# A gated delta-rule layer on one core: the last head pair's output projection, its loads and its buffers

## The chip, the cores and the metric

The kernel runs on 1 core of one Trainium2 chip. The time is the device time of one execution in microseconds (us). All data is float32.

## The reference

The layer normalizes `x` (2 sequences of 2048 tokens, 512 features) and adds three things: `x` itself, an attention part and a mixture of experts on the first 512 tokens. The change is in the attention part, which is a gated delta rule with 16 heads of 128 features:

```
q, k, v = silu(conv4(xn @ Wq)), silu(conv4(xn @ Wk)), silu(conv4(xn @ Wv))
alpha, beta = sigmoid(xn @ Wa + ba), sigmoid(xn @ Wb + bb)
for t:                                       # for every sequence and head
    err = S @ k[t] - v[t]
    S = alpha[t] * S - beta[t] * outer(err, k[t])
    o[t] = S @ q[t]
o = layernorm(o) * ln_w + ln_b
o = o * sigmoid(xn @ Wg)
out = x + o.reshape(T, 16 * 128) @ Wo + experts
```

## The kernel before

**Tiling.** A sequence is cut into 16 chunks of 128 tokens, four chunks make a block of 512. The heads are taken in pairs, eight pairs for each of the two sequences. The recurrence of a pair runs over the 16 chunks in order; within a chunk it is matrix products (a triangular inverse, products with the state S).

**Steps.** `recurrence(b, first)` runs over all chunks of all pairs of sequence `b`, and two steps more at the end to drain what is begun. In each step it weaves generators together by hand, `step(g)` advancing one of them: `before` (chunk m: scores, inverse; L614 loads, L625 scores), `after` (chunk m-1: L687 state times keys, L698, L707, state L714, outputs L721 and L724), `output` (chunk m-2: layer norm, transposition L753, gate, L759, and at L761 the store of the pair's outputs to `oT_d[b][ci]`), and the projections q, v and g of the next block (`item`, matmuls L155, convolution L141). In all but the last two pairs of the second sequence it also prepares the keys of the pair after next (`key_item`). In the last pair there are no keys, and in its last block no projections either.

**Order.** In the recurrence TensorE, VectorE, ScalarE and GpSimd keep the order that is written. The DMAs, issued by SyncE's queue (SP), are ordered by a scheduler by when they are expected to be ready; SP issues them one after another and stands still where one has to wait. The product `qg` on GpSimd (L388) reads `gin`, loaded at L380 into one buffer.

**Output projection.** All heads of a chunk, stored by the eight pairs in `oT_d[b][ci]` (128 x 16 x 128, 1 MB), are multiplied by Wo: 16 matmuls of 128x512 that add up in one PSUM bank, in four groups of four heads (each matmul is two instructions in the profile, so a group is x8). VectorE adds `x` (the tile `xf`), and the sum is stored in `out`. For the first sequence this runs behind its recurrence, for the second within the last pair's steps: at step ci of the last pair, from ci = 4 on, `out_chunk(b, ci - 4, ...)` issues the loads of `oTf` (L880) and `xf` (L882) and gives the four groups (L892) to the step, the first of them near its start. The tile `oTf` is a buffer of the ring that held the transposed input, `xT`, four buffers; one becomes free for it at ci = 4, one more at 8 and at 12:

```
if c == 0:
    slots.append(big())
...
last = out_chunk(b, ci - 4, wos, slots[ci % len(slots)])
```

Chunks 12 to 15 come behind the last step. The weights Wo take other buffers that are free by then (`load_wo`): two of the three of the ring `xA`, one of `xT`, and those of keys and inverses.

## Time and profile before

| what | us |
|---|---|
| median of 3 runs | 3907.49 |
| lowest, highest | 3904.68, 3910.8 |
| the profiled execution | 3906.37 |
| its span, first to last instruction | 3904.3 |
| last pair's step 4 (the first with outputs) begins | 3547.6 |
| last L687 (state times keys) | 3838.59 |
| last sum (L895) | 3900.56 |

The profile is of one execution. Engines are PE (TensorE's matmuls; PEld its weight loads), DVE (VectorE), ACT (ScalarE), POOL (GpSimd) and SP. A line of the timeline has the start and the duration in us, the engine, the line of the program, the operation, what it writes and reads, how many instructions are merged, and in brackets how long the engine was idle before and what ended that. PEclk is the TensorE clock that was granted, as a share of full speed. A line of the windows has the stretch, its length, and each engine's busy time with the number of its instructions.

### The profile page before, as it was taken

Reading aid. Unit: us, or ns where it says so; the run is one execution under the profiler, and the core shown is the slowest. Engines: PE = TensorE matmul, PEld = TensorE weight load, DVE = VectorE, ACT = ScalarE, POOL = GpSimd, SP = SyncE. Lnnn points to the kernel's source line nnn. Section 1 sums busy time; section 2 is a strip of 40 time slices with the busy share of each in tenths; the row PEclk is TensorE's granted clock in tenths of the full one; section 3 lists DMA queues with packets and bytes.
Section 4 is the critical chain, followed back from the end, with each engine's and each line's share of the span. In section 5 each row is a group of like instructions: output and inputs, shape, how many; then the busy total and the mean of one; then the engine's idle time right before and its main releaser. Section 6 shows DMA issues by size and latency. Waiting matters only on the chain.

```text
span 3904.3 us, 59006 instructions
## 1 busy us (share of the span) xinstructions
PE 3770.2 (97%) x18046; PEld 2461.4 (63%) x18046; DVE 2343.6 (60%) x6132; ACT 1701.5 (44%) x4027; POOL 1682.4 (43%) x3046
## 2 busy tenths in 40 slices
PE   7769999999999999999999999999999999998899
PEld 6437767677677766666654466666666666664454
DVE  5536656666666667777750177777777777763231
ACT  3424444444444445555520055555555555542110
POOL 1236546465564636363630053636363545541010
PEclk7789999999999999999999999999999999999999
DMA  4634665655666553545573435353435444342322
GB/s 133 209 98 143 185 169 154 195 158 175 168 176 172 159 178 107 143 132 169 147 240 117 120 103 137 107 139 109 132 111 139 119 127 126 103 111 72 100 75 89
DMA packets 579705, 541.36 MB, mean 139 GB/s; under 512 B 354688, under 2 KB 421760, under 8 KB 574272
## 3 DMA queue, kind: packets, MB, share of 16 engines
q1 hardware_dynamic: 557280, 456.18, 40.6%
q0 software_dynamic: 22112, 81.41, 7.1%
q8 instruction: 147, 2.41, 0.3%
q14 instruction: 166, 1.36, 0.1%
HBM read 363.69 MB, written 173.67 MB: 138 GB/s over the span
## 4 chain that ended last, share of the span: by engine, by line
PE 85%; DVE 6%; DMA 4%; issue 2%; POOL 2%; SPq 1%; ACT 1%; POOLq 0%; DVEq 0%; ACTq 0%
PE p L155 39%; PE p L892 11%; PE p L1044 4%; DVE cv L141 3%; PE o L721 3%; PE l L625 3%; PE p L205 3%; PE o L724 3%; PE c L698 3%; PE c L707 3%; PE c L687 2%; PE p L1059 2%; PE l L640 1%; PE l L658 1%; PE l L667 1%
## 5 line engine op out<-in xcount | busy, mean ns | idle before, releaser
L141 DVE SCALAR_TENSOR_TENSOR cv<-raw,prm,cv 128x512 f32<-128x512 f32 x1152 | 909.5, 790 | 106.2 <-ACT cv L136 44.1
L892 PE MATMUL p<-wo,oTf 128*128 128x512 f32 x1024 | 459.7, 604 | 26.3 <-DMA oTf<-oT_d 25.1
L155 PE MATMUL p<-xT,wq 128*128 128x512 f32 x1024 | 484.6, 596 | 0.0
L653 POOL COPY inv<-iT 32x32 f32<-32x32 f32 x512 | 103.1, 201 | 884.4 <-DVE iT L645 685.1
L155 PE MATMUL p<-xT,wg 128*128 128x512 f32 x1024 | 482.0, 594 | 0.0
L155 PE MATMUL p<-xT,wv 128*128 128x512 f32 x1024 | 481.0, 593 | 0.0
L735 POOL TENSOR_TENSOR rs<-rs,mhalf 128x2 f32<-128x2 f32 x256 | 270.2, 1055 | 485.4 <-DVE rs L734 481.1
L132 ACT COPY raw<-p 128x512 f32<-128x512 f32 x384 | 223.4, 582 | 533.2 <-PE p L155 515.0
L155 PE MATMUL p<-xT,wk 128*128 128x512 f32 x896 | 433.5, 610 | 0.0
L702 ACT COPY w<-c 128x256 f32<-128x256 f32 x256 | 95.3, 372 | 635.0 <-PE c L698 635.0
L714 DVE SCALAR_TENSOR_TENSOR S<-S,gtot,c 128x128 f32<-128x128 f32 x480 | 145.2, 344 | 356.6 <-PE c L707 342.5
L892 PEld LDWEIGHTS p<-wo,oTf 128*128 128x128 f32 x1024 | 193.9, 194 | 252.2 <-issue 223.8
L267 POOL TENSOR_TENSOR Y<-Y,t 128x30 f32<-128x30 f32 (+14 forms) x480 | 308.4, 643 | 37.2
L136 ACT ACTIVATE cv<-p,prm 128x512 f32<-128x512 f32 x384 | 300.4, 782 | 1.7
L264 POOL TENSOR_TENSOR t<-Y 128x30 f32<-128x30 f32 (+14 forms) x480 | 286.2, 596 | 8.8 <-DMA Y<-aT_d 2.3
L155 PEld LDWEIGHTS p<-xT,wq 128*128 128x128 f32 x1024 | 178.0, 192 | 135.8 <-issue 135.8
L155 PEld LDWEIGHTS p<-xT,wg 128*128 128x128 f32 x1024 | 176.8, 191 | 132.3 <-issue 132.1
L155 PEld LDWEIGHTS p<-xT,wv 128*128 128x128 f32 x1024 | 176.3, 191 | 132.0 <-issue 132.0
L691 DVE SCALAR_TENSOR_TENSOR r<-c,gd,kv 128x128 f32<-128x128 f32 x480 | 145.3, 344 | 166.2 <-PE c L687 165.1
L155 PEld LDWEIGHTS p<-xT,wk 128*128 128x128 f32 x896 | 160.6, 198 | 126.3 <-issue 126.3
L388 POOL TENSOR_TENSOR qg<-q,gin 128x512 f32<-128x512 f32 x128 | 194.1, 1516 | 98.6 <-ACT q L386 98.6
L707 PEld LDWEIGHTS c<-w,kg 128*128 128x128 f32 x1024 | 154.1, 191 | 121.4 <-issue 102.1
(172 smaller groups left out, 7145.8 us busy)
## 6 DMA issues: line engine op xcount, KB each, us to landing
row<-a_d SPq DMA_DIRECT2D x128, 258.0 KB
dec_d<-decA SPq DMA_DIRECT2D x128, 258.0 KB
decB<-dec_d SPq DMA_DIRECT2D x64, 516.0 KB
k_d<-kf SPq DMA_DIRECT2D x128, 256.0 KB
k<-k_d SPq DMA_DIRECT2D x64, 512.0 KB
gin<-gin_d SPq DMA_DIRECT2D x128, 256.0 KB
aT_d<-aTf SPq DMA_DIRECT2D x128, 256.0 KB
oT_d<-oT SPq DMA_DIRECT2D x256, 128.0 KB
```

Of the source, the lines that this page charges most:

```text
L132: nc.scalar.copy(raw[:, KS - 1:], ps)
L136: nc.scalar.activation(cv, ps, AF.Identity, bias=cbias(p, h0 + h), scale=tap(p, h0 + h, KS - 1))
L141: nc.vector.scalar_tensor_tensor(cv, raw[:, j:j + BLK], tap(p, h, j), cv, ALU.mult, ALU.add)
L155: nc.tensor.matmul(ps, lhsT=w[:, k, h * D:(h + 1) * D], rhs=xt[k], start=(k == 0), stop=(k == NKT - 1))
L264: nc.gpsimd.tensor_tensor(t, bass.AP(col.tensor, col.offset, [col.ap[0], (Q, j), (0, n)]), bass.AP(row.tensor, row.offset, [row.ap[0], (0, ...
L267: nc.gpsimd.tensor_tensor(Y[:, 0:j, j + 1:], Y[:, 0:j, j + 1:], t, ALU.add)
L388: nc.gpsimd.tensor_tensor(qg[:, h, :], qt[:, h, :], gin, ALU.mult)
L691: nc.vector.scalar_tensor_tensor(r[:, h, :], pq[:, h * D:(h + 1) * D], gd0[b][:, ci, h0 + h:h0 + h + 1], kv[:, 1, h, :], ALU.mult, ALU.add)
L707: nc.tensor.matmul(pss[:, h * D:(h + 1) * D], lhsT=kg[:, h, :], rhs=w[:, h, :], start=True, stop=True)
L735: nc.gpsimd.tensor_tensor(rs, rs, mhalf[:, 0:HG], ALU.pow)
L892: nc.tensor.matmul(py, lhsT=oT[:, h, :], rhs=wos[h], start=(h == 0), stop=(h == H - 1))
L1044: nc.tensor.matmul(ps[:fn, s, :], lhsT=w[f][:, s, k, :], rhs=xt[:, k, :], start=(k == 0), stop=(k == NKT - 1))
```

## The change

Three things are changed. First, the loads of a chunk's outputs and of its `x` are taken out of `out_chunk` into a function `get_out`, which is called one step earlier: at step ci, from ci = 3 on, it asks for chunk ci - 3, and the matmuls of chunk ci - 4 are given to the step. Second, there are two buffers in turn from the start: for even chunks three pieces (`pieces`: 8 heads in the third buffer of `xA`, and twice 4 heads in the two buffers of `decA`, which held the decay matrices of keys), each loaded by its own DMA; for odd chunks the tile `big` as before. Third, the two draining steps take chunks 12 and 13, and only chunks 14 and 15 come behind the last step. The first sequence's outputs use the same functions with one whole tile, in the order of before.

```diff
-                    if u == NB * NP - 1:
-
-                        if ci == 1:
-                            wos = load_wo(b)
-                        if ci >= 4:
-                            if c == 0:
-                                slots.append(big())
-                            for _ in last:
-                                pass
-                            last = out_chunk(b, ci - 4, wos, slots[ci % len(slots)])
-                            step(last)
                 A, B = pair
                 ps = None
+                if m >= len(steps) - NC and b == NB - 1:
+
+                    ci = m - len(steps) + NC
+                    if ci == 1:
+                        wos = load_wo(b)
+                    if ci == 3:
+                        slots.append(pieces())
+                    if ci == 4:
+                        slots.append([(big(), H)])
+                    for _ in last:
+                        pass
+                    last = none
+                    if ci > 3:
+                        last = out_chunk(b, ci - 4, wos, *got)
+                    if ci >= 3:
+                        got = get_out(b, ci - 3, slots[(ci - 3) % 2])
...
         if slots:
-            for ci in range(NC - 4, NC):
-                for _ in out_chunk(b, ci, wos, slots[ci % len(slots)]):
-                    pass
+            for c in range(NC - 2, NC):
+                if c > NC - 2:
+                    got = get_out(b, c, slots[c % 2])
+                drain(out_chunk(b, c, wos, *got))
...
-    def out_chunk(b, c, wos, oT):
-
-        nc.sync.dma_start(out=oT, in_=oT_d[b][c])
+    def pieces():
+
+        return [(half("oTa", [P, 8, C]), 8),
+                *((ap.tile([P, 4, C], F32, tag="decA", name="oTa", bufs=2), 4) for _ in range(2))]
+
+    def get_out(b, c, parts):
+
+        heads = []
+        for t, n in parts:
+            o = len(heads)
+            nc.sync.dma_start(out=t, in_=oT_d[b][c][:, o:o + n, :])
+            heads += [t[:, h, :] for h in range(n)]
         xin = ap.tile([P, HID], F32, tag="aTf", name="xf", bufs=2)
         nc.sync.dma_start(out=xin, in_=x[b, c * C:(c + 1) * C, :])
+        return heads, xin
+
+    def out_chunk(b, c, wos, heads, xin):
+
...
-        yield
         py = bank(ps_p, "p")
         for h in range(H):
-            nc.tensor.matmul(py, lhsT=oT[:, h, :], rhs=wos[h], start=(h == 0), stop=(h == H - 1))
+            nc.tensor.matmul(py, lhsT=heads[h], rhs=wos[h], start=(h == 0), stop=(h == H - 1))
```

More of the change, by code (lines that the diff above doesn't have):

```diff
@@ L899, in block_kernel @@
     recurrence(0, p0)
-    slots = [big() for _ in range(NBK - 1)]
+    slots = [[(big(), H)] for _ in range(NBK - 1)]
     wos, first = load_wo(0), projection(NP * NBK)
     for c in range(NC):
-        for _ in out_chunk(0, c, wos, slots[c % 3 if c < 12 else 1 + c % 2]):
-            pass
+        drain(out_chunk(0, c, wos, *get_out(0, c, slots[c % 3 if c < 12 else 1 + c % 2])))
         if c > 12:
```

## The prediction

> **What bounds the kernel now.** I read the page's busy shares and chain first, then TensorE's waits in the last 400 us, then that stretch cut at the chunks of the last pair, then TensorE's and SP's timelines there. The page:

> ```profile
> PE 3770.2 (97%) x18046; PEld 2461.4 (63%) x18046; DVE 2343.6 (60%) x6132; ACT 1701.5 (44%) x4027; POOL 1682.4 (43%) x3046
> PE 85%; DVE 6%; DMA 4%; issue 2%; POOL 2%; SPq 1%; ACT 1%; POOLq 0%; DVEq 0%; ACTq 0%
> L892 PE MATMUL p<-wo,oTf 128*128 128x512 f32 x1024 | 459.7, 604 | 26.3 <-DMA oTf<-oT_d 25.1
> ```

> TensorE is 97% busy and 85% of the chain that ended last, so time comes out only by removing TensorE work or its gaps. The output projection (L892) has idle time of its own: 26.3 us, 25.1 of it for the load of oTf. The waits of TensorE from 3540 us on say how many gaps these are:

> ```profile
> PE p L892 <- DMA oTf<-oT_d: 25.1, 6, 9.0
> ```

> Six gaps. To find what one costs with all that follows from it, I cut the last pair from the score product (first L625) of one chunk to that of the next:

> ```profile
> core 0: us, PE busy (x) PEld busy (x) DVE busy (x) ACT busy (x) POOL busy (x), PEclk, DMA share, GB/s
> 3547.60:3580.83 33.23, 24.23 (x81) 12.81 (x80) 6.45 (x20) 4.91 (x12) 3.73 (x7) 0.85 0.19 60
> 3580.83:3612.62 31.79, 26.64 (x90) 14.02 (x88) 7.59 (x23) 4.81 (x12) 3.86 (x8) 0.95 0.24 72
> 3612.62:3639.15 26.53, 23.31 (x81) 12.44 (x80) 6.45 (x20) 4.74 (x12) 1.90 (x5) 0.94 0.16 60
> 3639.15:3670.56 31.41, 26.73 (x90) 14.03 (x88) 7.58 (x23) 4.86 (x12) 2.46 (x6) 0.95 0.32 91
> 3670.56:3696.62 26.06, 23.31 (x82) 12.45 (x80) 6.46 (x20) 4.69 (x12) 3.54 (x6) 0.93 0.35 126
> 3696.62:3721.40 24.78, 24.78 (x90) 13.30 (x88) 7.58 (x23) 4.81 (x12) 3.67 (x7) 1.00 0.24 84
> 3721.40:3742.76 21.36, 21.36 (x82) 11.79 (x80) 6.47 (x20) 4.74 (x12) 1.71 (x4) 1.00 0.21 71
> ```

> The rows are chunks 4 to 10. Chunks 9 and 10 are solid: length equals TensorE's busy time, granted clock 1.00. They are the measure of a step without a gap: 24.78 us with two projection items (odd chunks), 21.36 with one (even). Chunks 4 to 8 do the same work in 26 to 33 us, at clocks of 0.85 to 0.95. No other engine is near full (DVE 7.6 of 25). Inside chunk 5, and in chunk 9 without the wait:

> ```profile
> 3580.83 0.69 PE L625 MATMUL l<-q,k 128*128 128x128 f32 x4
> 3586.67 5.29 PE L892 MATMUL p<-wo,oTf 128*128 128x512 f32 x8 [5.15 <-DMA oTf<-oT_d]
> 3591.80 1.88 PE L155 MATMUL p<-xT,wq 128*128 128x512 f32 x4
> ...
> 3696.62 0.69 PE L625 MATMUL l<-q,k 128*128 128x128 f32 x4
> 3697.15 3.60 PE L892 MATMUL p<-wo,oTf 128*128 128x512 f32 x8
> 3700.58 1.88 PE L155 MATMUL p<-xT,wq 128*128 128x512 f32 x4
> ```

> The wait is 5.15 us, and the eight matmuls behind it take 5.29 instead of 3.60. L625 to L155 takes 10.97 us against 3.96: 7.01 lost, two thirds of it idle and the rest slow clock. SP shows why some chunks wait and others don't:

> ```profile
> 3580.44 0.34 SPq L880 DMA_DIRECT2D oTf<-oT_d  x1
> 3699.05 0.33 SPq L882 DMA_DIRECT2D xf<-in_x  x1
> 3699.67 0.32 SPq L880 DMA_DIRECT2D oTf<-oT_d  x1
> ```

> Chunk 5's load leaves SP at 3580.44, when its one buffer has just come free, and TensorE wants it at 3581.5; 1 MB needs until 3586.7. From chunk 8 on there are more buffers: the load issued at 3699.67 is for chunk 10, whose outputs begin at 3721.9, 22 us later.

> **The change, part by part.**

> *Five gaps.* The load for the outputs of chunk ci-4 is now asked at step ci-1, into the other of two buffers. The first buffer is an 8-head piece (the third xA buffer) and two 4-head pieces (decA, which keys no longer use); the second is the tile that was the only one at steps 4 to 7. What goes is what each step has above the solid ones: 33.23 - 21.36 = 11.87; 31.79 - 24.78 = 7.01; 26.53 - 21.36 = 5.17; 31.41 - 24.78 = 6.63; 26.06 - 21.36 = 4.70. Sum 35.4 us: 24.8 of idle (9.00 + 5.15 + 3.22 + 4.68 + 2.75) and 10.6 of slow clock.

> *Clock, row and rule.* The rows have the slow clock behind all five gaps, also those of 3.22 and 2.75 us. [...] These very matmuls are in the trace, so I take the row.

> *Are the new loads in time?* Even chunks: heads 0 to 7 and 8 to 11 wait only for TensorE to be done with the same piece two chunks earlier (mid-step), heads 12 to 15 for the last pair's store of that chunk, issued at the step's end. Odd chunks: 1 MB, asked just behind that store. All are wanted one step later, 17.9 us at the least (the steps without projections, L625 at 3767.53 and 3785.44). The longest comparable load is the one of 7.2 us (issue 3550.08, matmul 3557.28). Cost taken: nothing, under a cover of over 10 us.

> *A new wait on SP.* Before, the load at step ci read a chunk stored a full step earlier; now it reads one stored just before. [...] The trace has this wait at the end:

> ```profile
> 3856.97 0.32 SPq L761 DMA_DIRECT2D oT_d<-oT  x1
> 3859.35 0.32 SPq L880 DMA_DIRECT2D oTf<-oT_d  x1
> ```

> 2.4 us, with SP stopped in it. Were it on the path in each of 13 chunks, it would take 31 us and leave 9 of the gain. But SP stops there already: xf waits 2.0 us for the store of out (3697.0 to 3699.05) in the same place, so the two overlap. Queued behind are inv for a chunk three steps on, gin and, twice, a block's operands. gin issued at 3579.17 feeds the POOL product at 3607.95, 29 us later. Cost taken: 0; bounds 0 and 31.

> *SP's extra issues.* Eight even chunks are three DMAs instead of one: 16 issues of 0.33 us, 5.3 us of SP in 300. Two of chunk 0's pieces move some pairs ahead, since those heads are stored then; each may hold SP for up to 2.4 us among key and operand loads, in stretches where TensorE has no wait. Cost 0; bounds 0 and 10. The bytes are the same. TensorE's order of instructions is unchanged up to the last chunk, and so is POOL's to the end.

> *The end.* Before, chunks 12 to 15 came behind the recurrence, and the two draining steps ran bare:

> ```profile
> 3840.34 0.68 PE L698 MATMUL c<-r,inv 128*128 128x128 f32 x4 [1.14 <-DVE r L691]
> ```

> From L687 at 3838.59 to the last matmul's end at 3900.5 is 61.9 us. The work in it, at the full clock's pace: 128 matmuls x 0.43 = 55.0; L687, L698 and L707 0.44 each; L721/L724 0.89; two L753 0.44. Sum 57.7. The change puts chunk 12's and 13's matmuls between the links of these chains, as the solid steps have them, so I take the difference, 4.2 us. What is late next there is chunk 15's load: its outputs are stored behind chunk 13's sum, 34.1 us after that L687 (chunks 12 and 13 27.5, three heads of chunk 14 that stand ahead 2.6, the links 2.7, the sum on DVE 0.7, the outputs' own last product 0.4, SP 0.2); the store ends at 36.6, the load lands 5.5 to 6.5 later at 42.1 to 43.1, and TensorE wants it at 43.9. In time by about 1 us; cost 0, bounds 0 and 4 (a gap with its slow clock).

> *Sum.* 35.4 + 4.2 = 39.6 us off a span of 3904.3: 3864.7. The profiled execution took 3906.37, 2.1 above its span: 3866.8. The median 3907.49 is 1.1 above that execution: 3867.9 us, 1.0% less than before.

> **The rivals.**

> *The loads come late in part.* SP takes its instructions in order, and the pieces wait for TensorE in mid-step. If half the gaps survive at 3 us with the slow clock behind (6 x 2.5 = 15 us), or chunk 15 is late and SP's holds show, the gain is 20 to 28 us: 3880 to 3888. For it: the 1 us margin at the end. Against: covers of over 10 us everywhere else. 12%.

> *It doesn't do what it says.* If each load were held until its step begins, only the 4.2 us at the end remain: 3903, no change. Against: the buffer asked for has been free since the step before, and the store that it waits for comes a whole step ahead of the use. 3%.

> *Slower, by POOL.* gin stands behind the pieces on SP. If it lands after POOL has reached the product qg, POOL stands still with the copies into inv and kg behind it, and L698 and L707 wait for those. A late gin can cost a step, up to 25 us, and three of them lie in this stretch: 75 - 40 = 35 us slower, 3943. It decides once gin is later than its use, that is, over 26 us later than now; the pieces hold SP for 14 at most, to the third group of outputs. 5%.

> **How the numbers follow.** The forecast has 80%, the rivals 12, 3 and 5. About 0.2% (7.8 us) is what a measurement of this kernel can tell from no change. Faster: 80 + 12 = 92%; same 3%; slower 5%. The low end is the forecast less the scatter of the runs shown, twice its 3 us above and below their median, and less 2 for gaps sized too small: 3860. The high end takes in the end's 4 us, SP's 10 and the near part of the first rival: 3884.

> **What would show it.** The chunks 4 to 8 of the last pair at 21.4 and 24.8 us in turn, clock 1.00; no TensorE wait on oTf or the pieces; loads issued a step ahead, about 2.7 us after each step's store of out; from the last chunk's L687 to the end of the matmuls some 58 us. Wrong would be: waits of L698 or L707 on POOL, a piece's load as TensorE's releaser, a gap before chunk 15, or a stretch ahead of 3540 us that changed its length.

## The result and the profile after

The changed kernel takes 3866.95 us (median of 4 runs, 3865.86 to 3868.41) against 3907.44 us before (4 runs, 3904.68 to 3910.8): a ratio of 0.9898, with a 95% interval of 0.9882 to 0.9914. The forecast was 3867.9. The span of the profiled execution went from 3904.3 to 3864.4 us. From the page after, its busy shares, its chain by engine and the output projection (now L910):

```profile
PE 3759.2 (97%) x18046; PEld 2457.7 (64%) x18046; DVE 2343.3 (61%) x6132; ACT 1701.4 (44%) x4027; POOL 1681.2 (44%) x3046
PE 85%; DVE 5%; issue 2%; DMA 1%; ACT 1%; POOL 0%; SPq 0%; POOLq 0%; ACTq 0%; DVEq 0%
L910 PE MATMUL p<-wo,oTf 128*128 128x512 f32 x768 | 335.1, 592 | 0.0
```

The number of matmuls is the same and TensorE is busy for 11.0 us less: the same instructions ran faster. The group's idle time of 26.3 us is 0.0, and DMA went from 4% of the chain to 1%. (The other 256 instructions read the pieces, `oTa`, and are a group of their own.) The steps 4 to 8 of the last pair (the prediction's "chunks 4 to 8"; the outputs made in them are those of chunks 0 to 4), cut at the score products as before; the first columns are the stretch, its length and TensorE's busy time, and PEclk is the granted clock:

```profile
core 0: us, PE busy (x) PEld busy (x) DVE busy (x) ACT busy (x) POOL busy (x), PEclk, DMA share, GB/s
3547.29:3568.64 21.35, 21.35 (x82) 11.78 (x80) 6.45 (x20) 4.92 (x12) 3.73 (x7) 1.00 0.42 132
3568.64:3593.42 24.78, 24.78 (x90) 13.30 (x88) 7.58 (x23) 4.81 (x12) 3.86 (x8) 1.00 0.19 63
3593.42:3614.76 21.34, 21.34 (x81) 11.77 (x80) 6.45 (x20) 4.74 (x12) 1.90 (x5) 1.00 0.32 109
3614.76:3639.54 24.78, 24.78 (x89) 13.30 (x88) 7.59 (x23) 4.86 (x12) 2.46 (x6) 1.00 0.32 86
3639.54:3660.89 21.35, 21.35 (x81) 11.78 (x80) 6.45 (x20) 4.69 (x12) 3.54 (x6) 1.00 0.39 139
```

In all five TensorE has no gap: length equals busy time, clock 1.00. They take 113.60 us against 149.02 before, 35.42 less. The whole difference of the spans can be laid out so. Ahead of step 4, 3547.60 became 3547.29, 0.3 less. Steps 4 to 8 give 35.4. From step 9 to the last L687 it is 141.97 us in both, no difference. From that L687 to the end of the span, 65.7 became 61.5, 4.2 less. Sum 39.9.

At the end, chunk 12's groups stand between the links of the last chain (L698, L707), which had waited for DVE and ACT before, and the chunks follow with no wait:

```profile
3802.86 0.61 PE L687 MATMUL c<-S,k 128*128 128x128 f32 x4
3803.31 3.60 PE L910 MATMUL p<-wo,oTa 128*128 128x512 f32 x8
3806.74 0.61 PE L698 MATMUL c<-r,inv 128*128 128x128 f32 x4
3807.19 3.60 PE L910 MATMUL p<-wo,oTa 128*128 128x512 f32 x8
3810.62 0.61 PE L707 MATMUL c<-w,kg 128*128 128x128 f32 x4
...
3835.58 11.32 PE L910 MATMUL p<-wo,oTa 128*128 128x512 f32 x26
3846.74 13.90 PE L910 MATMUL p<-wo,oTf 128*128 128x512 f32 x32
```

On SP the new waits are there, and no TensorE wait follows from them: from 3540 us to the end the profile shows no wait of TensorE. SP's own waits in the last pair from 3540 us on, for the loads of outputs (L894) and of `x` (L897):

```profile
SPq L894 <- PE l L667: 37.1, 6, 6.8
SPq L894 <- PE p L910: 29.9, 8, 5.3
SPq L897 <- DMA out<-xf: 16.6, 14, 2.4
SPq L894 <- DMA oT_d<-oT: 1.8, 8, 0.4
```

The columns are the total, the number of times and the longest. SP stands still for 67 us until TensorE has moved on (31.9 us in before, for L880). By the program a piece can be loaded only when TensorE has read the one before it in the same buffer. The profile names an output product (L910) for 29.9 us of this; for 37.1 us it names L667, a product that stands next to an output group. The wait that the forecast had bounded at 31 us, for the store of the outputs just made, is 1.8 us in all: SP has already stood for the store of `out` in the row above it.

### The profile page after: what moved, and what is told of

It reads as the page before. It is cut to its first block, busy times and chain, and to the rows that moved or that the text cites. A ratio compares the mean times of both kernels' runs of the same rounds, so it can differ in the third digit from the quotient of the medians.

```text
span 3864.4 us, 59038 instructions
## 1 busy us (share of the span) xinstructions
PE 3759.2 (97%) x18046; PEld 2457.7 (64%) x18046; DVE 2343.3 (61%) x6132; ACT 1701.4 (44%) x4027; POOL 1681.2 (44%) x3046
## 4 chain that ended last, share of the span: by engine, by line
PE 85%; DVE 5%; issue 2%; DMA 1%; ACT 1%; POOL 0%; SPq 0%; POOLq 0%; ACTq 0%; DVEq 0%
PE p L155 40%; PE p L910 11%; PE p L1061 4%; DVE cv L141 3%; PE o L721 3%; PE l L625 3%; PE p L205 3%; PE o L724 3%; PE c L698 3%; PE c L707 3%; PE c L687 3%; PE p L1076 2%; PE l L658 1%; PE l L640 1%; PE l L667 1%
## 5 line engine op out<-in xcount | busy, mean ns | idle before, releaser
L155 PE MATMUL p<-xT,wq 128*128 128x512 f32 x1024 | 482.7, 594 | 0.0
L155 PE MATMUL p<-xT,wg 128*128 128x512 f32 x1024 | 482.0, 594 | 0.0
L155 PE MATMUL p<-xT,wv 128*128 128x512 f32 x1024 | 481.0, 593 | 0.0
L155 PE MATMUL p<-xT,wk 128*128 128x512 f32 x896 | 436.4, 613 | 0.0
L910 PE MATMUL p<-wo,oTf 128*128 128x512 f32 x768 | 335.1, 592 | 0.0
L155 PEld LDWEIGHTS p<-xT,wq 128*128 128x128 f32 x1024 | 177.4, 191 | 134.4 <-issue 134.4
L155 PEld LDWEIGHTS p<-xT,wg 128*128 128x128 f32 x1024 | 176.8, 191 | 132.3 <-issue 131.9
L155 PEld LDWEIGHTS p<-xT,wv 128*128 128x128 f32 x1024 | 176.3, 191 | 132.0 <-issue 132.0
L910 PEld LDWEIGHTS p<-wo,oTf 128*128 128x128 f32 x768 | 143.5, 190 | 168.8 <-issue 168.6
L691 DVE SCALAR_TENSOR_TENSOR r<-c,gd,kv 128x128 f32<-128x128 f32 x480 | 145.2, 344 | 168.7 <-PE c L687 167.4
L155 PEld LDWEIGHTS p<-xT,wk 128*128 128x128 f32 x896 | 162.2, 199 | 128.6 <-issue 128.6
L707 PEld LDWEIGHTS c<-w,kg 128*128 128x128 f32 x1024 | 154.3, 191 | 121.2 <-issue 101.4
```

The costliest lines, as they stand in the source:

```text
L155: nc.tensor.matmul(ps, lhsT=w[:, k, h * D:(h + 1) * D], rhs=xt[k], start=(k == 0), stop=(k == NKT - 1))
L691: nc.vector.scalar_tensor_tensor(r[:, h, :], pq[:, h * D:(h + 1) * D], gd0[b][:, ci, h0 + h:h0 + h + 1], kv[:, 1, h, :], ALU.mult, ALU.add)
L707: nc.tensor.matmul(pss[:, h * D:(h + 1) * D], lhsT=kg[:, h, :], rhs=w[:, h, :], start=True, stop=True)
L910: nc.tensor.matmul(py, lhsT=heads[h], rhs=wos[h], start=(h == 0), stop=(h == H - 1))
```

## The experiments

They ran in three rounds, each on a chip of its own, and each with the kernel before beside it. Its medians are 3903.38 us (round 1: the late call, the two ends, the filled waits), 3904.06 us (round 2: one buffer, the waits filled in part, each load twice) and 3905.66 us (round 3: the changed kernel). Differences are taken to the kernel before of the same round. The changed kernel takes 40.4 us less than before in its round; where a kernel of another round is set against it, the 2 us between the chips are in the comparison.

**The changed kernel once more, and the loads called for in the step of use.** The first is unchanged; the second has this edit (and its like behind the loop):

```diff
                     if ci > 3:
+                        got = get_out(b, ci - 4, slots[ci % 2])
                         last = out_chunk(b, ci - 4, wos, *got)
-                    if ci >= 3:
-                        got = get_out(b, ci - 3, slots[(ci - 3) % 2])
```

> The changed kernel itself once more, on the chip of the experiments, as their measure. Theory A (the calling place of the loads is worth nothing, the difference between the two chips is the same for both kernels): as the kernel with the loads called for in the step that uses them, 3864 us within 2, and 39 to 40 less than before on the same chip. Rival (asking ahead in the program is worth a few microseconds beyond the second buffer): 3861 or less.

> The changed kernel, with the loads called for in the step that uses them, as before; the two buffers in turn and the new end stay. Theory A (what took the gaps away is the second buffer: SP's queue is ordered by readiness, and a load goes out as soon as its buffer is free and its chunk stored, wherever it is called): same as the changed kernel, 3867 us within 3. Theory B (asking a step ahead is what matters): the gaps come back at each step, about 7 us in each of 12, 3940 or more; at the least the 35 us of the five steps, 3902.

Measured: the changed kernel 3865.22 us, ratio to before 0.9899 (0.9882 to 0.9915); with the loads called for late 3864.37 us, ratio 0.9905 (0.9889 to 0.992). That is 40.4 and 39.0 us less than before, with intervals that overlap almost whole; in neither does TensorE wait in the last pair from 3540 us on. In the second one SP still issues the load of chunk 3 (3593.14) at the beginning of step 6, for matmuls in step 7:

```profile
3590.48 0.36 SPq L913 DMA_DIRECT2D out<-xf  x1
3590.89 0.42 SPq L761 DMA_DIRECT2D oT_d<-oT  x1
3592.56 0.33 SPq L896 DMA_DIRECT2D xf<-in_x  x1
3593.14 0.32 SPq L893 DMA_DIRECT2D oTf<-oT_d  x1
```

So the program's place for the call is worth nothing that these runs can tell. The load goes out a step ahead of its call, and what the change brings is the second buffer, from step 4 on. (That the scheduler goes by when the buffer is free is inferred from this order, and was not tested apart.)

**One buffer throughout.** The kernel before, without the second and third buffer:

```diff
-                            if c == 0:
+                            if ci == 4:
                                 slots.append(big())
```

> The kernel before with one buffer for oTf throughout: no second one at step 8, no third at step 12. Theory A (one buffer is what makes the gap: the load can start only when the last matmul of the chunk before has read it, and 1 MB takes 5 to 6 us): the gap comes at every further step, 9 to 15, at 5 to 7 us each with its slow clock (42), and at the end between chunks 12 to 15, three more at about 8 (24): 40 to 70 us slower than before, 3943 to 3973 on a chip where before takes 3903, with TensorE waiting for oTf 14 to 16 times. Rival (the gaps of steps 4 to 8 come from the operand loads of the next blocks, which collide with them there and are absent later): at most two or three further gaps, under 20 us.

Measured: 3970.54 us, ratio to before 1.0168 (1.0151 to 1.0185), 66.5 us slower. TensorE's waits in the last pair:

```profile
PE p L892 <- DMA oTf<-oT_d: 70.0, 16, 9.2
PE c L698 <- issue: 1.6, 2, 1.1
```

Sixteen waits for sixteen chunks, 70.0 us where before had six and 25.1. The gap follows the buffer and not the neighbourhood of steps 4 to 8: the steps from 9 on have gaps of 2.6 to 5.1 us, steps 4 to 8 of the same run 2.6 to 9.2 us.

**Idle time against slow clock.** The kernel before with matmuls that do nothing useful in front of each of the five waits:

```diff
         py = bank(ps_p, "p")
+        for _ in range({0: 10, 1: 6, 2: 4, 3: 5, 4: 3}.get(c, 0) if b == NB - 1 else 0):
+            nc.tensor.matmul(py, lhsT=wos[0][:, 0:P], rhs=wos[1], start=True, stop=True)
```

> The kernel before with 28 matmuls added whose result is overwritten (weights by weights, into the bank that the outputs then start anew): 10, 6, 4, 5 and 3 of them ahead of the first outputs at steps 4 to 8, where TensorE waits for oTf, sized to fill the waits of 9.0, 5.15, 3.22, 4.68 and 2.75 us at 0.86 us each (the longest by 0.4 us less, the third and fourth within 0.4, the second level). Theory A (10.6 of the 35.4 us are slow clock behind the idle stretches): it is faster than before by 10.6 less about 1 for what overhangs, 3897 to 3898, with the first group of outputs at 3.6 us instead of 5.3 to 6.3. Rival (these groups are slow because of the transfer that has just landed or goes on beside them, not because TensorE was idle): no gain, 3907 to 3909, and the groups stay at over 5 us.

Measured: 3895.31 us, ratio 0.9981 (0.9973 to 0.9988): 8.1 us less than before, by the addition of 28 matmuls. Two of the steps on TensorE's timeline (the added matmuls are L892, the outputs L894):

```profile
3546.05 8.75 PE L892 MATMUL p<-wo 128*128 128x512 f32 x20
3555.45 3.70 PE L894 MATMUL p<-wo,oTf 128*128 128x512 f32 x8 [0.66 <-DMA oTf<-oT_d]
...
3631.85 4.46 PE L892 MATMUL p<-wo 128*128 128x512 f32 x10
3636.78 3.70 PE L894 MATMUL p<-wo,oTf 128*128 128x512 f32 x8 [0.48 <-DMA oTf<-oT_d]
```

The groups that took 6.33 and 5.38 us before take 3.70, with the same transfer landing at the same place in the step within 0.3 us. So the slow groups come from TensorE's idleness, not from the transfer. The granted clock is 1.00 in all five steps, and they take 140.05 us, 9.0 less than before's 149.02. The 1.6 us that are missing from 10.6 were not told apart: some fillers overhang, and the groups that start behind idle stretches of 0.24, 0.48 and 0.66 us take 3.70 instead of 3.60 us even at the full clock.

**The waits filled in part.** The same with 8, 4, 2, 3 and 2 matmuls.

> The kernel before with 19 matmuls added whose result is overwritten, 8, 4, 2, 3 and 2 of them ahead of the first outputs at steps 4 to 8: the waits are to be left at about 2.1, 1.7, 1.5, 2.1 and 1.0 us. Theory A (the clock falls behind idle stretches of over two microseconds, as behind the 2.75 of before, and not behind shorter ones): groups behind waits of under 1.5 us take 3.6 to 3.8 us; those near 2 us may be either. [...]

Measured: 3898.4 us in a single run, so only its trace is used. The five outputs behind the shortened waits:

```profile
3557.27 5.40 PE L894 MATMUL p<-wo,oTf 128*128 128x512 f32 x8 [2.92 <-DMA oTf<-oT_d]
3586.41 3.70 PE L894 MATMUL p<-wo,oTf 128*128 128x512 f32 x8 [2.40 <-DMA oTf<-oT_d]
3614.30 3.70 PE L894 MATMUL p<-wo,oTf 128*128 128x512 f32 x8 [1.12 <-DMA oTf<-oT_d]
3640.54 3.70 PE L894 MATMUL p<-wo,oTf 128*128 128x512 f32 x8 [2.04 <-DMA oTf<-oT_d]
3668.38 3.70 PE L894 MATMUL p<-wo,oTf 128*128 128x512 f32 x8 [1.08 <-DMA oTf<-oT_d]
```

The first wait came out longer than meant, at 2.92 us, and it alone had a slow group behind it, 5.40 us. Behind 2.40 us and less no group is slow here, and the groups behind the waits under 1.5 us (1.12 and 1.08) take 3.70, as expected.

**The end alone, and all but the end.** The kernel before with chunks 12 and 13 in the draining steps and its own loads:

```diff
-                    if u == NB * NP - 1:
+                if m >= len(steps) - NC and b == NB - 1:
...
-            for ci in range(NC - 4, NC):
+            for ci in range(NC - 2, NC):
```

(The lines left out move with the condition; each chunk keeps one of before's three buffers.)

> The kernel before with the new end alone: its own buffers and its own loads, but chunks 12 and 13 given to the two draining steps. Theory A: the five gaps stay, the bare chains are covered: 4.2 us less than before, 3903. Rival (the end gains only with the loads asked ahead): 3907.

and the changed kernel with the old end:

```diff
-                if m >= len(steps) - NC and b == NB - 1:
+                if at and m >= len(steps) - NC and b == NB - 1:
...
-            for c in range(NC - 2, NC):
-                if c > NC - 2:
+            for c in range(NC - 4, NC):
+                if c > NC - 4:
```

> The changed kernel with the old end: chunks 12 to 15 behind the last step, nothing woven into the two draining steps. Theory A (the new end is worth 4.2 us for covering the bare chains, and here chunk 13's load comes behind the last stores too): slower than the changed kernel by 4.2 us for the bare chains and by up to 5 more for a gap of 3 to 4 us with slow clock behind it ahead of chunk 13: 3871 to 3876. Rival (the end is worth nothing, all of the gain is in the five gaps): 3867.

Measured: the end alone 3899.91 us, ratio 0.9991 (0.9982 to 0.9999), 3.5 us less than before by the medians, against 4.2 expected. The interval alone would only just exclude no change, but the trace has the links covered and the size: from the last L687 to the end of the span it is 61.5 us, as in the changed kernel, where before has 65.7.

```profile
3837.86 0.61 PE L687 MATMUL c<-S,k 128*128 128x128 f32 x4
3838.31 3.60 PE L893 MATMUL p<-wo,oTf 128*128 128x512 f32 x8
3841.74 0.61 PE L698 MATMUL c<-r,inv 128*128 128x128 f32 x4
```

All but the end: 3873.33 us, ratio 0.9931 (0.9918 to 0.9945), 30.1 us less than before. The kernel with the late call, of the same round, has 39.0, so the old end costs 9.0 us by these medians. The trace has 7.6 us of it:

```profile
3815.47 0.68 PE L698 MATMUL c<-r,inv 128*128 128x128 f32 x4 [1.14 <-DVE r L691]
3816.71 0.68 PE L707 MATMUL c<-w,kg 128*128 128x128 f32 x4 [0.55 <-ACT w L702]
...
3820.84 0.65 PE L753 MATMUL c<-unit,o 128*128 128x128 f32 x2 [2.34 <-DVE o L748]
3823.54 15.44 PE L910 MATMUL p<-wo,oTf 128*128 128x512 f32 x32 [2.05 <-DMA oTf<-oT_d]
```

The gaps in these four lines are 6.1 us, more than before's 2.0 in the same place, and a chunk that takes 13.90 us at the full clock takes 15.44, at a granted clock of 0.90. One reason is chunk 12: though called for behind the last step, its 32 instructions (`oTa`) stand within step 15, ahead of the bare links:

```profile
3786.63 5.31 PE L910 MATMUL p<-wo,oTa 128*128 128x512 f32 x12
3796.27 4.45 PE L910 MATMUL p<-wo,oTa 128*128 128x512 f32 x10
3805.78 4.46 PE L910 MATMUL p<-wo,oTa 128*128 128x512 f32 x10
```

So this run is not before's end: chunk 12 is no longer there to cover the wait of L753 or chunk 13's load. That load leaves SP 3.6 us behind the last L687 in this run (3817.33) and in the changed kernel (3806.47) alike, but is wanted 7.8 us behind it here and 16.2 us there. The worth of the new end is therefore read from the end alone, 4.2 us; the 9.0 also hold what the old end costs beside the two buffers.

**Each load twice.** The changed kernel, every load of the second sequence's outputs issued two times:

```diff
-            nc.sync.dma_start(out=t, in_=oT_d[b][c][:, o:o + n, :])
+            for _ in range(1 + b):
+                nc.sync.dma_start(out=t, in_=oT_d[b][c][:, o:o + n, :])
```

> The changed kernel, in which each load of the second sequence's outputs is issued twice, the second behind the first's completion: the data land later by the length of one more load (about 5.5 us for 1 MB, 3 for a piece), SP is held for as long, and 16 MB more are moved. Theory A (covers of 10 us or more at every chunk but the last, and about 1 us at chunk 15): no wait of TensorE at chunks 0 to 14, and at chunk 15 a gap of 4 to 5 us with about 1.9 of slow clock: 4 to 8 us slower than the changed kernel. Rival (the covers are thin, and SP's holds reach gin and the inverses, POOL and TensorE behind them): gaps at most steps, 20 us or more.

Measured: 3869.02 us, ratio to before 0.9913 (0.9897 to 0.993), 35.0 us less than before. The changed kernel has 40.4 in its round, and 3.8 us separate the two medians; the intervals overlap. TensorE has one wait for a load in the last pair:

```profile
3835.96 11.32 PE L911 MATMUL p<-wo,oTa 128*128 128x512 f32 x26
3849.43 14.00 PE L911 MATMUL p<-wo,oTf 128*128 128x512 f32 x32 [2.15 <-DMA oTf<-oT_d]
```

It is chunk 15, as expected; the other fifteen have covers that take a second load whole. The size was missed: 2.15 us instead of 4 to 5, and no slow clock behind it (14.00 us for 32 against 13.90). Two loads one after the other take 9.9 us here (issue 3839.52, matmul 3849.43), so one takes about 4.95, an estimate; the prediction's sum had put 5.5 to 6.5.

## Why the prediction was right

**Five gaps, 35.4 us.** Measured 35.4, and the five steps each came down to the 21.36 or 24.78 us that the solid steps had shown. The division was right in the main: filling the waits with idle work gave 9.0 us of the 10.6 put to the slow clock, and the busy time fell by 11.0. The forecast took the slow clock from the rows, also behind the two shortest gaps, 3.22 and 2.75 us, where it makes 3.9 us of the 10.6 (5.17 - 3.22 and 4.70 - 2.75). A fill that left a wait of 2.92 us had a slow group behind it again, 5.40 instead of 3.60 us. There is some luck in how close it came: the 10.6 are those of one execution. In the run with the end alone, which has the same five gaps, the third group took 3.70 us behind 2.88 us of idle time, where before had 5.40 behind 3.22.

**What took them away.** The forecast put it to the load being asked a step earlier into a second buffer. Of the two, the runs show the buffer alone: called for late, the loads leave as early, and with one buffer every chunk has its gap. The earlier call is the part of the account that was wrong, and it did not show in the number because the buffer came with it. The trace before had it already: the load for step 10, shown in the prediction, left SP at 3699.67, 22 us ahead of its use, though that kernel called for it in step 10 itself.

**The new wait on SP, 0 with bounds 0 and 31.** 1.8 us on SP, nothing on the path. The overlap with the wait for `out` was the right reason.

**The pieces on SP.** The forecast had them hold SP for 14 us at most, to the third group of outputs. In the steps without projections the second piece leaves about 14 us into the step; with them it is later. At step 6 SP issues the two pieces from 3603.78 to 3611.05, and that end lies 17.6 us into the step. It cost nothing: `gin`, issued at 3566.97, is used at 3588.74, 21.8 us later. Before had 28.8. The margin shrank by 7.0 us, and not because of the pieces: `gin` leaves SP 1.7 us ahead of step 5 in both kernels, and step 5 is 7.0 us shorter. The rival by POOL stayed far off; in the last pair POOL waits for no load.

**The end, 4.2 us.** 4.2 in the spans; done alone, 4.2 in the trace and 3.5 by the medians. Within it, chunk 15's margin was mis-sized: the load is issued at 3839.58 and wanted at 3846.74, and takes about 4.95, so it has 2.2 us and not about 1. The time of the issue was right (36.7 us behind the last L687, against 36.6); the load's length was the term that was off.

**The sum.** Span 3864.4 against 3864.7; median 3866.95 against 3867.9.

## What to carry to other kernels

Cut the trace at a point that recurs in every step, and take the solid steps as the measure of the others: the difference holds the wait and what follows from it (here 10.6 us of slow clock behind 24.8 of idle). Where a scheduler orders the DMA queue by readiness, look for the buffer that a load waits for before moving the call; one buffer more was worth 35 us here, the earlier call nothing that could be measured. The chain at the end of this pipeline was bare; independent matmuls that had to come anyway were laid between its links, for 4.2 us.

## What the runs showed of the hardware

Shorter waits close to each other had a slow clock behind them too, though not each time. At the end of before, waits of 1.14 and 0.55 us, with one group of products between them, were followed by this; a pair of products of one size takes 0.39, then 0.64 us:

```profile
3842.09 0.39 PE L721 MATMUL o<-w,pT 128*128 128x128 f32 x2
3842.57 0.64 PE L721 MATMUL o<-w,pT 128*128 128x128 f32 x2
```

With one buffer, waits of 1.09 and 0.55 us in the same place left it at 0.39. In the changed kernel with the old end, waits of 2.34 and 2.05 us with a few products between them had a granted clock of 0.90 behind them (32 matmuls in 15.44 instead of 13.90 us), while the single wait of 2.15 us of the loads issued twice had no slow clock behind it (14.00).

What stays open: why a wait of 2.62 us costs 3 us of slow clock in one step and one of 2.93 nothing in another was not tried further.
